# Selective scan on one NeuronCore: the PSUM tiles of a unit's transposed products as two one-bank halves, four in turn

## The chip, the cores and the metric

The kernel runs on one core of a Trainium2 chip. The metric is the device time of one execution in microseconds (us), taken as the median of several runs. Profile lines name the engines as PE (TensorE matmul), PEld (TensorE weight load), DVE (VectorE), ACT (ScalarE), POOL (GpSimd) and SP (the queue that issues the DMAs); L1633 is line 1633 of the kernel.

## What is computed

The input is a batch of 8 images of 64 x 64 positions and 192 channels, fp32. Layer 0 is a Mamba-like block with convolutions, a chunked state-space sum and an MLP; the change does not touch it. Layer 1 is a two-dimensional selective scan. Cut to what matters, for each image, each of 4 directions k, each of 384 channels d and each of 16 states n:

```
delta = softplus(dts + bias)                  # [4096 positions, 384]
dA    = exp(delta[..., None] * A[None])
dBu   = (delta * u)[..., None] * bm[:, :, None, :]
h     = dA * h + dBu                          # one position after another, 4096 of them
y     = sum over n of h * cm
```

Directions 0 and 2 go through the image by rows, forward and backward, 1 and 3 by columns. The four results are added, normalised, gated and projected, and the result is added to the layer's input.

## The kernel before

**Order of the program.** `tile_kernel` runs layer 0 for all images and then layer 1. `layer1` treats the images one after another. For each it runs first the "front" of this image (normalisation, projection, depthwise convolution, and the first pieces of its scan) beside the "finish" of the image before; the order of that part comes from a small planner (`Flow`) that gives each step a cost and a due time. Then it runs `main()` of `scan`, whose order is written out by hand: every instruction that goes through `o(...)` keeps program order on its engine.

**Tiling of the scan.** The 4096 positions of a direction are cut into 8 chunks of TT = 512. A step s is one chunk of one direction: 32 steps for an image. The 16 states are handled as NP1 = 8 pairs p, and the 384 channels as DT = 3 blocks d of 128. A unit u is one (s, p, d): 24 units in a step, 768 in an image, 6144 in all. A tile of a unit has 128 partitions, which are 2 states x 64 channels, and two halves f = 0, 1, one for each 64 channels of block d; each half is 512 positions long.

**What a unit does, engine by engine.**

- ScalarE: `decay` (L1606) writes ea = exp(delta x A), 2 instructions of 128 x 512, one for each f. `weigh` (L1591) writes pw, the products delta x u x B with the positions on partitions, 8 instructions for each (s, p), handed out 3, 3, 2 to the units d = 0, 1, 2, and ten instructions ahead of their use.
- TensorE: `supply` (L1617) turns pw round, 8 transposes of 128 x 128: four (j) for half 0 and then four for half 1. They go into the PSUM tile g. `collect` (L1662, with L1660 for the first pair of direction 0) sums the states of the unit before into the PSUM tile y of its channel block.
- VectorE: `run` (L1633) scans, 2 instructions of 128 x 512, one for each f. Each reads ea from SBUF and g from PSUM and writes hs. `add` (L1671, L1673) takes y into the image's sum after the last pair.
- GpSimd: a small copy cy (L1645) keeps the last column as the start of the next step, and hc = hs x C (L1647), one instruction of 128 x 1024, is what `collect` reads.
- SP: the DMAs that repeat delta (dr) and C (cb) over the partitions, and the loads for the next step (xc, ut).

**The loop.** In `main`, iteration u issues in this order: run(u), decay(u + 2), the 2 or 3 weigh of this iteration, supply(u + 1), collect(u - 1), add(u - 2), and then the pieces of `prepare` for the next step that are due at this unit. Those pieces (delta, its transposes p_du and p_b, the projections p_d at L1480, the copies xdbl at L1487 and bt at L1503, and softplus spa at L1516 and L1517) are dealt out by a table over the unit's place in the step: p_d at 2, 3 and 4, xdbl at 5, p_b at 6, and so on.

**Buffers.** The pool of ea (e1) has 3 buffers, so decay(u + 2) takes the one that run(u - 1) read. hs and hc have 3 each, y has one for each of three channel blocks. In PSUM, [...]y takes 3 banks, the tile of `prepare` takes 1, and g takes 4: two tiles of two banks each. The tile g is `[128, 2, TT]` fp32, 4 KiB a partition, so half 0 lies in one bank and half 1 in the next. A tile's buffer is handed on when its readers are done with it; all waits between engines are derived from what reads and writes which tile.

Of the kernel before, what the change touches and what calls it, by code (L numbers as in the profile page):

```python
# [8 lines left out]
F32 = mybir.dt.float32  # L9
AF = mybir.ActivationFunctionType  # L10
ALU = mybir.AluOpType
PSUM = bass.MemoryType.PSUM
# [5 lines left out]
TT = 512  # L18
# [35 lines left out]
def bc(ap, axis, shape):  # L54

    return ap.unsqueeze(axis).to_broadcast(shape)
# [975 lines left out]
def layer1(tc, consts, x1s, mv1, out, w_in, w_x, w_dt, w_out):  # L1032
# [3 lines left out]
    kw = v["kw"].rearrange("p (t k) -> p t k", t=DT)  # L1036
# [3 lines left out]
    with ExitStack() as ctx:  # L1040
# [393 lines left out]
        def scan(xo):  # L1434
# [5 lines left out]
            pools, ready = {}, {}  # L1440

            def spool(name, bufs, **kw):
                pools[name] = cx.enter_context(tc.tile_pool(name=name, bufs=bufs, reuse_waits="tile", **kw))
# [4 lines left out]
            made = {}  # L1448

            def first(s):  # L1450
                return steps[s][1] == (0 if steps[s][0] < 2 else NS1 - 1)
# [123 lines left out]
            def load_c(s, p):  # L1575
                state[s]["cb", p] = cb = pools["bc1"].tile([128, TT], F32, name="cb")
                for i in range(2):
                    o(
                        nc.sync.dma_start(
                            out=cb[i * 64 : i * 64 + 64], in_=state[s]["cd"][2 * p + i].partition_broadcast(64)  # L1580
                        )
                    )

            def weigh(s, p, j, i):

                st = state[s]
                if i == 0:
                    st["pw", p, j] = pools["pw1"].tile([128, 2 * DT, 2, 64], F32, name="pw")
                n = 2 * p + i
                o(  # L1590
                    nc.scalar.activation(  # L1591
                        st["pw", p, j][:, :, i],
                        st["duT"][:, j].rearrange("p (g c) -> p g c", c=64),
                        AF.Copy,
                        scale=st["bt"][:, j, n : n + 1],
                    )
                )

            def decay(u):
                s, p, d = units[u]  # L1600
                k, c = steps[s]
                made["e", u] = ea = pools["e1"].tile([128, 2, TT], F32, name="ea")
                for f in range(2):
                    at = 2 * d + f
                    o(
                        nc.scalar.activation(  # L1606
                            ea[:, f], state[s]["dr", d][:, f], AF.Exp, scale=an[:, k, p, at : at + 1]
                        )
                    )

            def supply(u):
                s, p, d = units[u]
                made["g", u] = g = pools["g1"].tile([128, 2, TT], F32, name="g")
                for f in range(2):
                    for j in range(NB1):
                        o(
                            nc.tensor.transpose(  # L1617
                                g[:, f, j * 128 : j * 128 + 128],
                                state[s]["pw", p, j][:, 2 * d + f].rearrange("p a b -> p (a b)"),
                                ident,  # L1620
                            )
                        )

            def run(u):
                s, p, d = units[u]
                k, c = steps[s]
                st = state[s]
                ea, g = made.pop(("e", u)), made.pop(("g", u))
                h = pools["h1"].tile([128, 2, TT], F32, name="hs")
                rev = (lambda ap: ap) if k < 2 else (lambda ap: ap[:, ::-1])  # L1630
                for f in range(2):
                    o(
                        nc.vector.tensor_tensor_scan(  # L1633
                            rev(h[:, f]),
                            rev(ea[:, f]),
                            rev(g[:, f]),
                            0.0 if first(s) else state[s - 1]["cy"][:, p, d, f : f + 1],
                            ALU.mult,
                            ALU.add,
                        )  # L1640
                    )
                if "cy" not in st:
                    st["cy"] = pools["pr1"].tile([128, NP1, DT, 2], F32, name="cy")
                last = TT - 1 if k < 2 else 0
                o(nc.gpsimd.tensor_copy(st["cy"][:, p, d], h[:, :, last]))  # L1645
                made["hc", u] = hc = pools["h1"].tile([128, 2, TT], F32, name="hc")
                o(nc.gpsimd.tensor_mul(hc, h, bc(st["cb", p], 1, [128, 2, TT])))  # L1647

            def collect(u):
                s, p, d = units[u]  # L1650
                k, c = steps[s]
                st = state[s]
                if p == 0:
                    st["y", d] = pools["y1"].tile([128, TT], F32, name=f"y{d}")
                y = st["y", d]
                hc = made.pop(("hc", u))
                half = [slice(f * 64, f * 64 + 64) for f in range(2)]
                if p == 0 and k == 0:
                    for f in range(2):
                        o(nc.tensor.matmul(y[half[f]], dskip[:, d, half[f]], st["xc"][:, d], start=True, stop=False))  # L1660
                for f in range(2):
                    o(nc.tensor.matmul(y[half[f]], sel, hc[:, f], start=p == 0 and k > 0, stop=p == NP1 - 1))  # L1662

            def add(u):
                s, p, d = units[u]
                k, c = steps[s]
                if p == NP1 - 1:
                    ya = view(yacc, k, d, c * TT, TT)
                    yv = seq(state[s]["y", d], k)
                    if k == 0:  # L1670
                        o(nc.vector.tensor_copy(ya, yv))  # L1671
                    else:
                        o(nc.vector.tensor_add(ya, ya, yv))  # L1673
# [51 lines left out]
                f.at["du", d] = r  # L1725

            def main():
                for name, n, kw in (("h1", 3, {}), ("y1", 1, dict(space=PSUM)), ("g1", 2, dict(space=PSUM))):
                    spool(name, n, **kw)
                supply(0)  # L1730
                rest = iter(todo[10:])
                nu = len(units)
                for u, (s, p, d) in enumerate(units):
                    if p == 0 and d == 0:
                        pieces = prepare(s + 1) if s + 1 < len(steps) else {}
                    s2, p2 = (s, p + 1) if p < NP1 - 1 else (s + 1, 0)
                    if s2 < len(steps) and d == 0:
                        load_c(s2, p2)
                    run(u)
                    if u + 2 < nu:  # L1740
                        decay(u + 2)
                    for _ in range((3, 3, 2)[d]):
                        if t := next(rest, None):
                            weigh(*t)
                    if u + 1 < nu:
                        supply(u + 1)
                    if u >= 1:
                        collect(u - 1)
                    if u >= 2:
                        add(u - 2)  # L1750
                    for f, *args in pieces.get(p * DT + d, ()):
                        f(*args)
                collect(nu - 1)
                add(nu - 2)
                add(nu - 1)
                cx.close()
# [7 lines left out]
        for b in range(nb + 1):  # L1764

            f = Flow(tc, after=True)
# [126 lines left out]
```

## Time and profile before

| | |
|---|---|
| three runs, us | 23690.56, 23702.0, 23706.31 |
| median | 23702.0 |
| span of the profiled execution | 23706.3 (the highest of the three runs, to the tenth) |
| layer 0 | 0 to about 5000 us of the span |
| scan of one image, first transpose to last y (image 4 of 0 to 7) | 2105.9 |
| finish of an image and front of the next, between two scans | about 240 |
| ACT busy in that scan | 2079.1 |
| DVE busy in that scan | 2007.6 |
| POOL busy in that scan | 1918.6 |
| PE busy in that scan | 1864.9 |

A group's line in the profile gives source line, engine, operation, tiles written and read, shape, count, then busy us and mean ns of one, then the idle time of the engine just before these instructions and who ended most of it. A line of the order of time gives start, length, engine, line, operation, tiles and count, and in brackets the idle time before it with its releaser. A line of waits reads: who waited for whom, us in total, times, longest. Busy time of instructions that overlap on one engine is counted once in a busy table, but each keeps its own length in a mean.

### The profile page before, as it was taken

How to read it: one execution, taken by the hardware profiler on the slowest of the kernel's cores; microseconds unless marked ns; L12 is line 12 of the kernel's file. 1: busy time of each engine (PE TensorE's matmuls, PEld its weight loads, DVE VectorE, ACT ScalarE, POOL GpSimd, SP SyncE). 2: the span in 40 equal slices, each digit the busy share in tenths (PEclk: the TensorE clock that was granted, in tenths of full speed). 3: DMA queues.
4: the chain of work that ended last, by engine and by line, in shares of the span. 5: the costliest groups of instructions: out<-in, count | busy, mean ns of one | idle time of the engine just before them, and what ended most of it. 6: DMA issues, size and time to landing. Idle time of an engine off the chain costs nothing.

```text
span 23706.3 us, 312102 instructions
## 1 busy us (share of the span) xinstructions
PE 21012.6 (89%) x100356; PEld 10233.4 (43%) x100356; DVE 21257.2 (90%) x22093; ACT 20961.7 (88%) x37466; POOL 16001.1 (67%) x12871
## 2 busy tenths in 40 slices
PE   8999999978888888888888888888888888888888
PEld 4444444434444444444444444444444444444444
DVE  7888888779998999899989998999899989998998
ACT  5666666679998999899989998999899989998998
POOL 1111111159995998599859986997699769976997
PEclk8999999989999999999999999999999999999999
DMA  1111111133233322332233233322333333333332
GB/s 51 44 44 44 45 45 46 36 101 81 82 78 112 81 81 77 110 82 81 77 108 81 81 80 111 81 81 78 108 81 82 84 102 81 82 86 100 82 82 67
DMA packets 1205983, 1859.70 MB, mean 78 GB/s; under 512 B 268960, under 2 KB 502336, under 8 KB 1195136
## 3 DMA queue, kind: packets, MB, share of 16 engines
q1 hardware_dynamic: 1204352, 1839.73, 28.5%
q8 instruction: 807, 13.22, 0.2%
q14 instruction: 824, 6.75, 0.1%
HBM read 1225.98 MB, written 210.50 MB: 61 GB/s over the span
## 4 chain that ended last, share of the span: by engine, by line
POOL 46%; PE 22%; ACT 13%; DVE 8%; issue 6%; DMA 3%; SPq 1%; POOLq 0%; ACTq 0%; DVEq 0%
POOL hc L1647 43%; ACT pw L1591 5%; ACT ea L1606 5%; POOL cy L1645 3%; PE p_f L955 3%; DVE xs L1201 2%; DMA xc<-xo 2%; PE p_x L448 2%; PE p_f L975 2%; PE y L1662 2%; PE p_o L872 1%; PE g L1617 1%; PE p_y L789 1%; PE p_d L1480 1%; PE p_z L531 1%
## 5 line engine op out<-in xcount | busy, mean ns | idle before, releaser
L1647 POOL TENSOR_TENSOR hc<-hs,cb 128x1024 f32<-128x1024 f32 x6144 | 14577.6, 2373 | 12.3 <-POOL cy L1645 10.5
L1633 DVE TENSOR_TENSOR_SCAN hs<-ea,cy,g 128x512 f32<-128x512 f32 x10752 | 13027.1, 1262 | 602.4 <-PE g L1617 408.7
L1591 ACT ACTIVATE pw<-duT,bt 128x384 f32<-128x384 f32 x16384 | 8875.4, 601 | 23.5 <-DVE duT L1538 23.5
L1606 ACT ACTIVATE ea<-dr,an 128x512 f32<-128x512 f32 x12288 | 8121.7, 709 | 186.9 <-DVE hs L1633 169.5
L1662 PE MATMUL y<-hc,sel 128*64 128x512 f32 x24576 | 6628.6, 618 | 1836.3 <-POOL hc L1647 1816.1
L1617 PEld LDWEIGHTS g<-ident,pw 128*128 128x128 f32 x49152 | 5288.2, 141 | 4335.1 <-issue 2666.3
L1617 PE MATMUL g<-ident,pw 128*128 128x128 f32 x49152 | 6788.1, 279 | 60.8 <-ACT pw L1591 29.3
L1645 POOL COPY cy<-hs 128x2 f32<-128x2 f32 x6144 | 1150.7, 187 | 3394.4 <-DMA out_x<-xl 1744.8
L1662 PEld LDWEIGHTS y<-hc,sel 128*64 128x64 f32 x24576 | 1226.6, 135 | 3250.6 <-POOL hc L1647 3025.0
L1633 DVE TENSOR_TENSOR_SCAN hs<-ea,g 128x512 f32<-128x512 f32 x1536 | 1764.2, 1203 | 160.9 <-PE g L1617 119.6
L365 POOL TENSOR_TENSOR s<-xs 96x512 f32<-96x512 f32 x64 | 121.7, 1902 | 2136.0 <-DVE xs L343 1846.6
L1201 DVE SCALAR_TENSOR_TENSOR xs<-pad,p,xs 128x4096 f32<-128x4096 f32 x192 | 860.9, 4484 | 48.0 <-ACT xs L1191 40.8
L1509 PE MATMUL p_dt<-xdbl,wd 13*128 13x512 f32 x1536 | 857.5, 639 | 41.8 <-DVE de L1522 39.9
L365 POOL TENSOR_TENSOR s<-sq 96x512 f32<-96x512 f32 x128 | 180.4, 1409 | 937.9 <-ACT sq L378 842.3
L1480 PE MATMUL p_d<-xc,wx 128*44 128x512 f32 x1536 | 788.7, 596 | 23.4 <-DMA xc<-xo 23.4
L343 DVE SCALAR_TENSOR_TENSOR x<-xx,p,x 96x512 f32<-96x512 f32 x1024 | 784.4, 815 | 15.2 <-ACT x L332 15.0
L955 PE MATMUL p_f<-h,wf 96*128 96x512 f32 x1536 | 757.2, 631 | 43.8 <-ACT zs L550 27.4
L343 DVE SCALAR_TENSOR_TENSOR xs<-xin,p,xs 96x512 f32<-96x512 f32 x1024 | 746.9, 768 | 3.6 <-ACT xs L332 3.6
L975 PE MATMUL p_f<-m,wf 128*96 128x512 f32 x1536 | 695.0, 603 | 0.0
L1531 PEld LDWEIGHTS p_du<-ident,de 128*128 128x128 f32 x3072 | 323.4, 141 | 610.1 <-DVE de L1522 406.3
L365 POOL TENSOR_TENSOR s<-x 96x512 f32<-96x512 f32 x64 | 109.1, 1704 | 690.3 <-DVE x L343 606.7
L448 PE MATMUL p_x<-h,wi 96*128 96x512 f32 x1024 | 559.4, 679 | 12.0 <-ACT h L405 12.0
(202 smaller groups left out, 19293.3 us busy)
## 6 DMA issues: line engine op xcount, KB each, us to landing
cb<-cd SPq DMA_DIRECT2D x4096, 128.0 KB
dr<-de SPq DMA_DIRECT2D x3072, 128.0 KB
xc<-xo SPq DMA_DIRECT2D x256, 768.0 KB
e<-csd SPq DMA_DIRECT2D x256, 384.0 KB
xl<-x SPq DMA_DIRECT2D x256, 384.0 KB
ut<-xo SPq DMA_DIRECT2D x128, 768.0 KB
ut<-xo SPq DMA_DIRECT2D x256, 384.0 KB
xo<-xs SPq DMA_DIRECT2D x48, 1024.0 KB
```

What stands on the lines that cost most here:

```text
L343: nc.vector.scalar_tensor_tensor(im(out[:, ct]), tap(ct, j), w[:, ct, j : j + 1], im(out[:, ct]), ALU.mult, ALU.add)
L448: nc.tensor.matmul(ps, wi[:, ct, 390 + mt * 128 : 518 + mt * 128], h[:, ct], start=ct == 0, stop=ct == 1)
L955: nc.tensor.matmul(ps, wf1[:, ct, mt * 128 : mt * 128 + 128], h[:, ct], start=ct == 0, stop=ct == 1)
L975: nc.tensor.matmul(ps[:CP], wf2[:, kt, ct * CP : ct * CP + CP], m[:, kt], start=kt == 0, stop=kt == 5)
L1201: nc.vector.scalar_tensor_tensor(xs, tap(j), kw[:, d, j : j + 1], xs, ALU.mult, ALU.add)
L1591: nc.scalar.activation(st["pw", p, j][:, :, i], st["duT"][:, j].rearrange("p (g c) -> p g c", c=64), AF.Copy, scale=st["bt"][:, j, n : n + 1],
L1606: nc.scalar.activation(ea[:, f], state[s]["dr", d][:, f], AF.Exp, scale=an[:, k, p, at : at + 1])
L1617: nc.tensor.transpose(g[:, f, j * 128 : j * 128 + 128], state[s]["pw", p, j][:, 2 * d + f].rearrange("p a b -> p (a b)"), ident,)
L1633: nc.vector.tensor_tensor_scan(rev(h[:, f]), rev(ea[:, f]), rev(g[:, f]), 0.0 if first(s) else state[s - 1]["cy"][:, p, d, f : f + 1], ALU ...
L1645: o(nc.gpsimd.tensor_copy(st["cy"][:, p, d], h[:, :, last]))
L1647: o(nc.gpsimd.tensor_mul(hc, h, bc(st["cb", p], 1, [128, 2, TT])))
L1662: o(nc.tensor.matmul(y[half[f]], sel, hc[:, f], start=p == 0 and k > 0, stop=p == NP1 - 1))
```

## The change

The pool g1 gets four buffers for two, and a unit takes two tiles `[128, TT]` (one bank each), one for each half, for one tile `[128, 2, TT]`. With four in turn, half f of unit u + 1 takes the buffer that half f of unit u - 1 had. The tile of half 1 is asked for after the transposes of half 0 have been issued. `run` takes a list of the two tiles. The number and order of instructions on each engine, their shapes and the four banks stay.

```diff
             def supply(u):
                 s, p, d = units[u]
-                made["g", u] = g = pools["g1"].tile([128, 2, TT], F32, name="g")
                 for f in range(2):
+                    made["g", u, f] = g = pools["g1"].tile([128, TT], F32, name="g")
                     for j in range(NB1):
                         o(
                             nc.tensor.transpose(
-                                g[:, f, j * 128 : j * 128 + 128],
+                                g[:, j * 128 : j * 128 + 128],
                                 state[s]["pw", p, j][:, 2 * d + f].rearrange("p a b -> p (a b)"),
                                 ident,
                             )
...
-                ea, g = made.pop(("e", u)), made.pop(("g", u))
+                ea, g = made.pop(("e", u)), [made.pop(("g", u, f)) for f in range(2)]
                 h = pools["h1"].tile([128, 2, TT], F32, name="hs")
                 rev = (lambda ap: ap) if k < 2 else (lambda ap: ap[:, ::-1])
                 for f in range(2):
...
                             rev(ea[:, f]),
-                            rev(g[:, f]),
+                            rev(g[f]),
                             0.0 if first(s) else state[s - 1]["cy"][:, p, d, f : f + 1],
...
-                for name, n, kw in (("h1", 3, {}), ("y1", 1, dict(space=PSUM)), ("g1", 2, dict(space=PSUM))):
+                for name, n, kw in (("h1", 3, {}), ("y1", 1, dict(space=PSUM)), ("g1", 4, dict(space=PSUM))):
```

## The prediction, made before the run

> **What bounds the kernel now.** I read the groups of the page first, then the busy table cut at step boundaries, then ScalarE's waits, then the order of time around one wait.
>
> The groups (line, engine, operation, tiles, count | busy us, mean ns | idle before, releaser):
>
> ```profile
> L1633 DVE TENSOR_TENSOR_SCAN hs<-ea,cy,g 128x512 f32<-128x512 f32 x10752 | 13027.1, 1262 | 602.4 <-PE g L1617 408.7
> L1591 ACT ACTIVATE pw<-duT,bt 128x384 f32<-128x384 f32 x16384 | 8875.4, 601 | 23.5 <-DVE duT L1538 23.5
> L1606 ACT ACTIVATE ea<-dr,an 128x512 f32<-128x512 f32 x12288 | 8121.7, 709 | 186.9 <-DVE hs L1633 169.5
> L1617 PE MATMUL g<-ident,pw 128*128 128x128 f32 x49152 | 6788.1, 279 | 60.8 <-ACT pw L1591 29.3
> ```
>
> VectorE waits for the transposed products (g) 408.7 us in all, and ScalarE waits for the scan (hs) 169.5 us. The question is which of the two sets the end. The busy table answers it (columns: PE, PE loads, DVE, ACT, POOL busy us, clock, DMA). I cut it from the ea of unit 14 of one step to that of the next: a step of direction 0, the step into direction 1, a later one.
>
> ```profile
> 7463.10:7529.59 66.49, 60.21 (x329) 29.21 (x330) 63.18 (x60) 65.35 (x120) 59.88 (x49) 1.00 0.28 80
> 7862.10:7927.35 65.25, 58.17 (x321) 28.88 (x321) 62.34 (x61) 65.15 (x120) 60.32 (x49) 1.00 0.34 82
> 8123.78:8189.29 65.51, 57.80 (x317) 28.47 (x318) 63.17 (x60) 65.33 (x119) 59.88 (x49) 1.00 0.32 82
> ```
>
> ScalarE bounds the scan: it is busy 65.15 of 65.25 us where it never waits, so **65.25 us is the floor of a step** with this ScalarE work. The other two steps are 1.24 and 0.26 us above it. Only that excess can be won; VectorE's 63 of 65.5 us is cover, not the bound. ScalarE's wait:
>
> ```profile
> ACT ea L1606 <- DVE hs L1633: 169.5, 102, 12.8
> ```
>
> Most of the 169.5 us is one wait of some 12.6 us in each image's first step, while TensorE still finishes the image before; the change doesn't touch that. The rest is the excess. One such wait, in step 1 of image 4:
>
> ```profile
> 12137.72 1.09 PE L1617 MATMUL g<-ident,pw 128*128 128x128 f32 x8
> ...
> 12138.95 2.45 DVE L1633 TENSOR_TENSOR_SCAN hs<-ea,cy,g 128x512 f32<-128x512 f32 x2 [0.79 <-PE g L1617]
> ...
> 12141.46 1.09 PE L1617 MATMUL g<-ident,pw 128*128 128x128 f32 x8
> ...
> 12142.69 2.45 DVE L1633 TENSOR_TENSOR_SCAN hs<-ea,cy,g 128x512 f32<-128x512 f32 x2 [1.29 <-ACT ea L1606]
> ...
> 12145.06 0.66 DVE L1487 COPY xdbl<-p_d 44x512 f32<-44x512 f32 x1
> 12145.17 1.33 ACT L1606 ACTIVATE ea<-dr,an 128x512 f32<-128x512 f32 x2 [0.97 <-DVE hs L1633]
> ```
>
> The eight transposes of unit 5 end at 12141.46 + 1.09 = 12142.55; both scans run from 12142.69 to 12145.14; the ea of unit 8, which takes the buffer that these scans read, starts at 12145.17, 0.97 us late. (The releaser named at 12142.69 is wrong: that unit's ea is older, and g ended 0.14 us before, as for unit 4.) So the first scan, which reads only half 0 of g, waited until half 1 was written too. Over all units that waited on g, the first scan starts 0.135 us after the eighth transpose, never after the fourth.
>
> **What the Trainium skill says.** "PSUM — Partial Sum Buffer", Terms, gives a bank as 2 KiB per partition (512 fp32) and forbids two engines on one bank and quadrant at once. A half tile is just one bank, so VectorE reads one while TensorE writes another; a unit's two halves already lie in two banks, so nothing here is newly shared. The trace agrees so far as its scans read while transposes of the next unit are written. "VectorE: DVE Perf Modes", Two Vector instructions with no wait between them, says that a wait which the sequencer handles alone does not hold up the next instruction. The trace agrees: four scans in a row took 4.79 us where 4 x 1.262 = 5.05, an overlap of 0.085 at each joint, also at the joint with an EVENT_SEMAPHORE (50 ns, one for nearly every unit now: 6137). "TensorE: Matmul & The Clock Gate", The cost: per-tile semaphore tail, says that matmuls end in order and that signals queue at 26 ns each. No run here shows that price.
>
> **The change part by part.**
>
> 1. *The first scan no longer waits for half 1.* Start times of single transposes: the first step is 0.165 us, the later six 0.109. Half 1 is thus 4 x 0.109 = **0.436 us**, and a first scan that waits on g starts up to that much earlier. The second scan starts 1.19 us after the first, when half 1 is long there.
>
>    Direction 0, steps 1 to 7 of each image: 66.50 us each (median over the images). The chain is the last pw of the second state pair, then TensorE without a gap for 8.3 us (dskip, y and p_d matmuls between the transposes), then the scans of unit 5, then ea. Only its last link gets shorter, by 0.436; the remaining 0.8 of the 1.25 stays, because TensorE is late next. 7 x 0.436 = 3.05 us an image.
>
>    Directions 1 to 3: 23 steps, of which three stand at 65.25, three at 65.34 and the others at about 65.56, some up to 65.9. There, too, units 4 and 5 wait on g (0.44 and 0.49 us by the trace), then the scans and a copy run in a row to unit 6, whose buffer ea of unit 9 needs. The visible idle there is only 0.08 us; the start-to-start times of pw and ea show the rest: 0.506 without a wait, 0.607 and 0.678 for these two, together 0.27 (a waited instruction loses its 0.1 us overlap). The shift of 0.436 covers that, so the step falls to the floor. Summing excess over 65.25, capped at 0.436, over all eight images: 48 us, 6.0 an image. It is 5.2 from the usual steps and 0.8 from the longer ones.
>
>    First step of an image: the first scan waits 0.18 us on g behind a copy, and gains that; the scan of unit 5 then gains 0.436 as above. 0.6 an image. End: the last six scans run in a row from one that waited 0.37 us on g; 0.36 an image.
>
>    Sum: 3.05 + 6.0 + 0.6 + 0.36 = 10.0 us an image, **80 us** for eight.
>
> 2. *Half 0 comes free after the first scan.* TensorE's transposes waited on the scan 8 times for 12.5 us in all, once an image: the third unit's, 1.64 us. Half 0 could start there about 1.2 us sooner, but y of unit 0 behind it waits for POOL's hc anyway. Cover gone, it would be 8 x 1.2 = 10 us; I take 0.
>
> 3. *The second scan needs a wait on TensorE of its own.* It now waits only for ea. Two waits make another EVENT_SEMAPHORE, 50 ns. Behind it in VectorE's queue are all later scans, and POOL's hc and ScalarE's ea wait for those. It is read while the first scan runs; I take 0. Upper bound: 0.05 plus the lost overlap 0.084 = 0.134 a unit. It can't be below 0.
>
> 4. *TensorE: a second wait and a second signal per unit.* Behind the wait stand half 1, then y. The wait is for a scan two units back, done unless the unit is among the 8 above. Units whose transposes wait on four pw tiles run eight in 1.09 us like the others, so a satisfied wait is free. Upper bound: 0.056 each, as at the first step of a unit (0.165 less 0.109). In direction 0 three supplies lie in the chain: 0.17 off 0.436, or 7 x 8 x 0.17 = 9 us. I take 0. The signal, at the skill's 26 ns, lies behind 0.135 us of latency per scan: up to 7 x 8 x 0.026 = 1.5 us, taken as 0.
>
> 5. *Space* is the same (four banks), and no step, DMA or order moves. Everything in part 1 removes a wait from an unchanged order on in-order engines; that alone can't make anything start later.
>
> The profiled execution's span is 23706.3 us, the same as the highest of the three runs (23706.31), so nothing lies around it; the median is 23702.0, 4.3 lower. 23706.3 - 80 = 23626; on the median, **23622 us**.
>
> **The rivals.**
>
> - *Only visible idle comes back.* If the lost overlap of 0.2 us a step stays, directions 1 to 3 give what the idle itself sums to, 19 us, not 48: 24 + 19 + 5 + 3 = 51 us, 23651. For it: idle is what a profile shows. Against: the step with no wait reaches 65.25 with the same instructions.
> - *The scan still waits for both halves*, because the signal is still given after the eighth transpose: 23702. For it: in the kernel before the halves were already in separate banks and it waited all the same. Against: the halves become separate tiles, and waits elsewhere go by tile.
> - *Slower: the wait of part 3 isn't hidden.* At 0.134 us a unit VectorE needs 24 x 0.134 = 3.2 us more a step, on 63.2 busy and some 0.7 of g waits left: 67.1. That is 1.6 above 65.5 for 23 steps and 0.6 above 66.5 for 8: (37 + 5) x 8 = 340 us, 24040. It is slower from about (65.5 - 63.9) / 24 = 0.07 us a unit. Against: the overlap that survives a sequencer wait today.
> - *More*: the 10 us of part 2 and uncapped long steps (3 us): 23609.
>
> **How the numbers follow.** The forecast 0.70 (23605 to 23640 by the bounds of parts 2 and 4), visible idle only 0.12, both halves 0.08, slower 0.06, more 0.04. A difference of 0.2% (47 us), about what a measurement of this kernel can tell from no change, lies at 23655. Faster by over it: 0.70 + 0.04 and half of the 0.12 rival or a little less, 0.79. Slower by over it 0.06; within, 0.15. The range goes from 23605 to 23672: forecast, more (nearly) and visible idle, with the bounds.
>
> **What would show it.** Scans that start about 0.135 us after a fourth transpose; direction-0 steps at 66.06 us; later steps at 65.25 with ScalarE's wait on the scan gone but for the first step; VectorE's EVENT_SEMAPHOREs near 12,288 with scans still overlapping by 0.085. Wrong if two scans of a unit lose that overlap, if first scans still start after the eighth transpose, or if later steps stay at 65.5 though scans start sooner: then something else holds ScalarE.

## The result, and the profile after

| | before | after |
|---|---|---|
| median, us (5 runs each) | 23702.0 | 23620.3 |
| ratio of after to before, 95% interval | | 0.9962 [0.9949, 0.9976] |
| span of the profiled execution | 23706.3 | 23594.7 |

The changed kernel is 0.38% faster by the ratio; 23622 was forecast. One of its five runs had a mean TensorE clock of 0.61 and took 35113.5 us; it is left out of the ratio, but not of the median, which without it is 23613.2. The gain is thus 88.8 us, with an interval from some 57 to 121 us; by the median in the table it would be 81.7.

The two profiled spans differ by 111.6 us, more than the medians. So I split them at the same instructions, summed over the eight images (the parts are given to a tenth, so sums can be off by one in the last digit). A step is measured as in the prediction, from the first ea of its unit 14 to that of the next.

| part of the span, us | before | after | difference | forecast |
|---|---|---|---|---|
| layer 0, to the first transpose of layer 1 | 5004.8 | 4982.0 | -22.8 | 0 |
| start of a scan to unit 14 of its first step | 301.4 | 296.5 | -5.0 | -5 |
| direction 0, 7 steps each | 3724.4 | 3700.1 | -24.4 | -24 |
| directions 1 to 3, 23 steps each | 12055.5 | 12004.5 | -51.0 | -48 |
| last step | 503.7 | 503.6 | -0.1 | 0 |
| from there to the last y of a scan | 267.8 | 263.9 | -3.9 | -3 |
| between scans, and after the last | 1848.8 | 1844.3 | -4.6 | 0 |

The scans give 84.3 us. Layer 0 has the same instructions in both kernels; in the profiled executions of the ten experiments it took 4988 to 5016 us. So I take its 22.8 us as scatter between executions, and compare kernels below by step times and by medians of runs. The median of each of the 31 steps of an image agrees within 0.02 us between the kernel before and experiment 1, which runs at the same speed.

The busy table of the changed kernel, for the same three steps as before (columns: PE, PE loads, DVE, ACT, POOL busy us, clock, DMA):

```profile
7429.72:7495.79 66.07, 60.54 (x330) 29.26 (x329) 62.91 (x60) 65.37 (x119) 59.85 (x49) 1.00 0.31 81
7826.15:7891.40 65.25, 59.15 (x326) 29.20 (x323) 61.92 (x60) 65.15 (x120) 60.62 (x49) 1.00 0.32 82
8087.11:8152.35 65.24, 58.44 (x318) 28.40 (x316) 63.04 (x60) 65.14 (x119) 59.83 (x49) 1.00 0.33 82
```

Direction 0 went from 66.50 to 66.07 and the later step from 65.51 to 65.24, with ScalarE busy for 65.14 of it: it stands on the floor. All 23 later steps of all images do (65.22 to 65.26); the steps that stood at 65.25 did not move.

The order of time at the place the prediction quotes (step 1 of the fourth image, which is image 3 where the first is image 0; units 4, 5 and 8):

```profile
12081.31 1.09 PE L1617 MATMUL g<-ident,pw 128*128 128x128 f32 x8
...
12082.11 2.45 DVE L1633 TENSOR_TENSOR_SCAN hs<-ea,cy,g 128x512 f32<-128x512 f32 x2 [0.82 <-PE g L1617]
...
12085.06 1.09 PE L1617 MATMUL g<-ident,pw 128*128 128x128 f32 x8
...
12085.85 2.45 DVE L1633 TENSOR_TENSOR_SCAN hs<-ea,cy,g 128x512 f32<-128x512 f32 x2 [1.29 <-PE g L1617]
...
12088.34 1.33 ACT L1606 ACTIVATE ea<-dr,an 128x512 f32<-128x512 f32 x2 [0.53 <-DVE hs L1633]
```

The first scan now starts 0.80 us after the first of its unit's eight transposes, where it took 1.23 (12137.72 to 12138.95), and before the eighth ends. It is so wherever the first scan of a unit waited on g: 602 did, and started 0.135 us after the fourth transpose ended (median); before, 788 did, and started 0.136 us after the eighth. ScalarE's wait at unit 8 fell from 0.97 to 0.53. The two scans still run together in 2.45 us. VectorE's own wait on g (0.82, was 0.79) did not shrink: the scans of unit 3 had finished sooner too, 0.02 us before the first transpose of unit 4, where before it was 0.44 after it. That is why one reads a step's length, not the wait.

The groups, the waits of ScalarE, and the EVENT_SEMAPHOREs on VectorE's sequencer at L1633 (these are waits of the scans; the three numbers are shortest, median and longest, in ns):

```profile
L1633 DVE TENSOR_TENSOR_SCAN hs<-ea,cy,g 128x512 f32<-128x512 f32 x10752 | 12939.0, 1261 | 381.4 <-PE g L1617 356.9
...
L1606 ACT ACTIVATE ea<-dr,an 128x512 f32<-128x512 f32 x12288 | 8118.4, 709 | 137.0 <-DVE hs L1633 132.5
```

```profile
ACT ea L1606 <- DVE hs L1633: 132.5, 79, 12.6
```

```profile
L1633 DVEq EVENT_SEMAPHORE  x11523: 21/21/1271, 4985.6 to 23453.8; - x199
```

The same in the kernel before:

```profile
L1633 DVEq EVENT_SEMAPHORE  x6137: 21/50/1654, 5009.2 to 23566.1; - x198
```

The added waits are there (11523 for 6137), and cost nothing that can be seen: a scan keeps its 1261 ns, and the two scans of a unit overlap by 0.084 us in the median, with a wait between them (3053 units) as without (3091).

What VectorE waited for g, and TensorE for GpSimd's hc, before:

```profile
DVE hs L1633 <- PE g L1617: 528.3, 788, 3.5
...
PE y L1662 <- POOL hc L1647: 1816.1, 3496, 1.4
```

and after:

```profile
DVE hs L1633 <- PE g L1617: 433.3, 602, 3.2
...
PE y L1662 <- POOL hc L1647: 1167.2, 2301, 1.6
```

### The profile page after: what moved, and what is told of

Its sections match the earlier page's. It is cut to its first block, busy times and chain, and to the rows that moved or that the text cites. A ratio compares the mean times of both kernels' runs of the same rounds, so it can differ in the third digit from the quotient of the medians.

```text
span 23594.7 us, 314377 instructions
## 1 busy us (share of the span) xinstructions
PE 21129.1 (90%) x100356; PEld 10211.3 (43%) x100356; DVE 21205.1 (90%) x22093; ACT 20933.3 (89%) x37466; POOL 15970.7 (68%) x12871
## 4 chain that ended last, share of the span: by engine, by line
ACT 55%; PE 22%; POOL 9%; DVE 7%; issue 4%; DMA 2%; SPq 1%; POOLq 0%; ACTq 0%; DVEq 0%
ACT pw L1591 27%; ACT ea L1606 23%; POOL hc L1647 8%; PE p_f L955 3%; DVE xs L1201 2%; PE p_x L448 2%; PE p_f L975 2%; ACT spa L1517 2%; PE g L1617 2%; PE p_o L872 1%; ACT spa L1516 1%; PE p_y L789 1%; PE y L1662 1%; PE p_z L531 1%; PE p_o L1407 1%
## 5 line engine op out<-in xcount | busy, mean ns | idle before, releaser
L1633 DVE TENSOR_TENSOR_SCAN hs<-ea,cy,g 128x512 f32<-128x512 f32 x10752 | 12939.0, 1261 | 381.4 <-PE g L1617 356.9
L1606 ACT ACTIVATE ea<-dr,an 128x512 f32<-128x512 f32 x12288 | 8118.4, 709 | 137.0 <-DVE hs L1633 132.5
L1617 PE MATMUL g<-ident,pw 128*128 128x128 f32 x49152 | 6991.4, 280 | 414.2 <-ACT pw L1591 394.9
L1633 DVE TENSOR_TENSOR_SCAN hs<-ea,g 128x512 f32<-128x512 f32 x1536 | 1759.4, 1202 | 113.9 <-PE g L1617 76.4
L1522 DVE SCALAR_TENSOR_TENSOR de<-spa,p_dt 128x512 f32<-128x512 f32 x768 | 520.0, 677 | 240.1 <-ACT spa L1517 240.0
```

Of the source, the lines that this page charges most:

```text
L1606: nc.scalar.activation(ea[:, f], state[s]["dr", d][:, f], AF.Exp, scale=an[:, k, p, at : at + 1])
L1617: nc.tensor.transpose(g[:, j * 128 : j * 128 + 128], state[s]["pw", p, j][:, 2 * d + f].rearrange("p a b -> p (a b)"), ident,)
L1633: nc.vector.tensor_tensor_scan(rev(h[:, f]), rev(ea[:, f]), rev(g[f]), 0.0 if first(s) else state[s - 1]["cy"][:, p, d, f : f + 1], ALU.mu ...
```

## The experiments

All edits are on the changed kernel unless it says otherwise, and are cut to what matters. Each ratio is to the kernel before, run beside the experiment. Step times are medians over the eight images, for the usual step of direction 0 and the usual later one; the kernel before has 66.50 and 65.56, the changed one 66.07 and 65.24.

**1. Half 1 first.** Is it the first scan's wait, or that buffers come free by halves?

```diff
-                for f in range(2):
+                for f in (1, 0):
                     made["g", u, f] = g = pools["g1"].tile([128, TT], F32, name="g")
```

> Keeps the four half tiles, their separate hand-on and the added waits, but issues the transposes of half 1 before those of half 0, so that the first scan is ready only after the eighth transpose again. Theory (the first scan used to wait for half 1): the whole gain is gone, 23702 within 15 us, direction-0 steps back at 66.5 and the usual later steps at 65.5 to 65.6. Rival (buffers that come free half by half, four in turn, are what helped): stays at about 23620, steps at 66.07 and 65.24.

Measured: ratio to the kernel before 0.9999 [0.9990, 1.0008]; steps 66.50 and 65.56. Its direction-0 and later steps, and the place of unit 5 and unit 8:

```profile
7473.61:7540.11 66.50, 60.22 (x331) 29.25 (x330) 63.20 (x60) 65.36 (x119) 59.89 (x49) 1.00 0.29 80
...
8134.22:8199.75 65.53, 57.78 (x319) 28.47 (x318) 63.19 (x60) 65.35 (x119) 59.89 (x49) 1.00 0.31 82
```

```profile
12154.89 1.09 PE L1617 MATMUL g<-ident,pw 128*128 128x128 f32 x8
...
12156.12 2.45 DVE L1633 TENSOR_TENSOR_SCAN hs<-ea,cy,g 128x512 f32<-128x512 f32 x2 [1.29 <-ACT ea L1606]
...
12158.61 1.33 ACT L1606 ACTIVATE ea<-dr,an 128x512 f32<-128x512 f32 x2 [0.96 <-DVE hs L1633]
```

The scan starts 1.23 us after the first transpose again and ScalarE waits 0.96. Half tiles, four in turn, hand-on by halves, all as in the change, and the gain is gone. So the gain hangs on the order of half 0 and half 1 against the scans. One thing is not as in the change, though the expectation says so: the added waits on VectorE are gone too, since the half that the second scan reads is now written first.

```profile
L1633 DVEq EVENT_SEMAPHORE  x6137: 21/50/2520, 5018.5 to 23578.6; - x198
```

So this run says nothing on what the added waits cost.

**2. Transposes in pairs.** Both half tiles are now asked for ahead of the transposes.

```diff
                 for f in range(2):
-                    made["g", u, f] = g = pools["g1"].tile([128, TT], F32, name="g")
-                    for j in range(NB1):
+                    made["g", u, f] = pools["g1"].tile([128, TT], F32, name="g")
+                for j in range(NB1):
+                    for f in range(2):
...
```

> Transposes issued in pairs, block j of half 0 and then block j of half 1, so that half 0 is written after the seventh transpose. Theory: a unit whose pw are all there gains only 0.109 us for its first scan. But a unit with d = 0 that waits for the last pw has two transposes left after it, not five, so that what stands behind it on TensorE starts 0.33 us sooner: direction-0 steps 66.50 - 0.33 - 0.11 = 66.06, later steps near the floor (65.25 to 65.3). About 23620 to 23630. Rival (only the place of the fourth transpose counts): 66.39 and about 65.45, 23675.

Measured: 0.9960 [0.9945, 0.9974], median 23621.5; steps 66.07 and 65.24. The time came as the theory had it, and excludes the rival's 66.39. It stands on two effects that happen to sum to the change's, so experiments 6 and 7 take them apart.

**3. Three halves in turn.**

```diff
-                for name, n, kw in (("h1", 3, {}), ("y1", 1, dict(space=PSUM)), ("g1", 4, dict(space=PSUM))):
+                for name, n, kw in (("h1", 3, {}), ("y1", 1, dict(space=PSUM)), ("g1", 3, dict(space=PSUM))):
```

> The changed kernel with three half tiles in turn, not four. Half 1 of a unit then takes the buffer that half 0 of the unit just before it had, so its transposes wait for that unit's first scan. Theory (number of buffers and early hand-on don't matter, the separate wait does): steps stay at 66.07 and 65.24, about 23620; at most a few waits of TensorE of under 1 us. Rival (hand-on matters): slower than 23650.

Measured: 0.9957 [0.9942, 0.9971], median 23611.7; steps 66.06 and 65.24. TensorE does wait for scans now:

```profile
PE g L1617 <- DVE hs L1633: 190.1, 308, 0.7
```

These 190 us (12.5 in the kernel before, 4.6 in the changed one) are cover: no step got longer. One bank of PSUM comes free at no cost.

**4. Pieces for the next step one unit later.**

```diff
-                    2: [(project, 0)],
-                    3: [(project, 1)],
...
-                    17: [(keep_du, 2)],
+                    3: [(project, 0)],
+                    4: [(project, 1)],
...
+                    18: [(keep_du, 2)],
```

> The changed kernel with the pieces for the next step (p_d projections to the last product) one unit later each. In direction 0 one p_d projection (0.86 us of TensorE) then falls behind the transposes of unit 5. Theory (after the change TensorE's gapless run is what is left of the excess, 66.07 - 65.25 = 0.82): direction-0 steps fall to the floor of 65.25 to 65.3, others stay; 23620 - 7 x 8 x 0.82 = 23574. Rival (VectorE or POOL holds direction 0 next): steps stay above 65.8, 23605 or more.

Measured: 0.9940 [0.9925, 0.9955], median 23575.2; direction 0 at 65.43, later steps at 65.24. The time is as forecast, the step not quite: 0.64 of the 0.83 us that were left in direction 0 are gone, and 0.19 stays. The edit moves VectorE's copy xdbl and all later pieces too, so this run alone does not say how much of the 0.64 was TensorE's gapless run; experiment 7 shows that the run alone gives 0.33. In the start-to-start times of ScalarE the 0.19 shows as two lost overlaps of 0.08 and 0.09 us, at units 10 and 11.

**5. Two halves in turn.**

```diff
-                for name, n, kw in (("h1", 3, {}), ("y1", 1, dict(space=PSUM)), ("g1", 4, dict(space=PSUM))):
+                for name, n, kw in (("h1", 3, {}), ("y1", 1, dict(space=PSUM)), ("g1", 2, dict(space=PSUM))):
```

> The changed kernel with only two half tiles, one for each half. The transposes of half 0 for the next unit then wait for the first scan of this unit, those of half 1 for its second. Theory (VectorE needs the next half 0 only 1.2 us after it gives the buffer back, and four transposes take 0.44): most units lose nothing; where p_d or dskip matmuls stand behind the late half 1, units 2 to 5 of a step, up to 0.5 us of VectorE, part of it seen by ScalarE: steps 65.3 to 65.6 and about 66.3, 23640 to 23720. Rival (buffers in turn are what the change is about): clearly slower than the kernel before, 23800 or more.

Measured: 1.0133 [1.0119, 1.0146], median 24021.0; steps 68.64 and 66.93. A miss: slower than I allowed, and the rival's sign. What VectorE and ScalarE wait for in it:

```profile
DVE hs L1633 <- PE g L1617: 882.0, 1458, 2.4
```

```profile
ACT ea L1606 <- DVE hs L1633: 387.6, 547, 12.5
```

VectorE waits on g 882 us (433 in the changed kernel). I had looked only at what VectorE needs. The transposes of half 1 must now wait for the second scan of the unit before, and TensorE, in order, keeps y, p_d and the next unit's half 0 behind them: in step 11 of the fifth image half 1 of units 1, 2, 3 and 7 ends 1.17 us after its half 0 instead of 0.44, and the scans of units 4, 5 and 8 then wait 0.95, 0.43 and 0.33 us for g. So the number of buffers does matter, down to two; three are enough.

**6. Pairs for all units with d = 0.** The pair order of experiment 2 where d = 0, half after half where not.

```diff
-                    made["g", u, f] = g = pools["g1"].tile([128, TT], F32, name="g")
-                    for j in range(NB1):
...
+                    made["g", u, f] = pools["g1"].tile([128, TT], F32, name="g")
+                fs, js = range(2), range(NB1)
+                for f, j in [(f, j) for j in js for f in fs] if d == 0 else [(f, j) for f in fs for j in js]:
...
```

> The changed kernel, transposes in pairs (block j of both halves) for units with d = 0 only, half after half for the others. Theory: TensorE's gapless run of direction 0 starts 3 x 0.109 = 0.33 us sooner after the last pw, and units 4 and 5 keep their 0.436: direction-0 steps 66.07 - 0.33 = 65.74, later steps at 65.24: 23620 - 18 = 23602. Rival (VectorE or POOL is next in direction 0): 66.07, 23620.

Measured: 0.9959 [0.9946, 0.9973], median 23611.6; direction 0 at 65.99: not 65.74 as expected, nor the rival's 66.07. ScalarE's wait at unit 8 fell from 0.53 to 0.21, as the theory had it, but one of 0.32 stood at unit 9, where there had been 0.07.

**7. Pairs for one unit.** This run tests why. The edit is shown against experiment 6.

```diff
-                for f, j in [(f, j) for j in js for f in fs] if d == 0 else [(f, j) for f in fs for j in js]:
+                for f, j in [(f, j) for j in js for f in fs] if (p, d) == (1, 0) else [(f, j) for f in fs for j in js]:
```

> The changed kernel, transposes in pairs for one unit of a step only, the one with p = 1, d = 0, at which TensorE's gapless run of direction 0 starts. The run with pairs for all d = 0 units took 0.32 us off ScalarE's wait at unit 8 but put 0.25 on at unit 9, whose buffer the scans of unit 6 read, and unit 6 has d = 0 too. Theory: with unit 6 half after half, the gain of 0.33 stays: direction-0 steps 65.72 to 65.76, 18 us less than the changed kernel. Rival (something else holds unit 9): 65.99 again.

Measured: 0.9951 [0.9934, 0.9968], median 23590.4; direction 0 at 65.74. As forecast. Both effects of experiment 2 are thereby seen apart: 0.33 us of TensorE's run that starts at unit 3, and 0.25 us more a step where unit 6 has the pair order too (experiment 6: its first scan follows the seventh transpose, not the fourth), 0.33 where all units have it (experiment 2).

**8. Experiments 4 and 6 together.**

```diff
-                    2: [(project, 0)],
...
+                    3: [(project, 0)],
...
-                    made["g", u, f] = g = pools["g1"].tile([128, TT], F32, name="g")
-                    for j in range(NB1):
...
+                    made["g", u, f] = pools["g1"].tile([128, TT], F32, name="g")
+                fs, js = range(2), range(NB1)
+                for f, j in [(f, j) for j in js for f in fs] if d == 0 else [(f, j) for f in fs for j in js]:
...
```

> The changed kernel with both: pairs for units with d = 0, and the pieces for the next step one unit later. Theory: what is left of the excess in direction 0 (65.43 - 65.24 = 0.19) is still the same run of TensorE, so it goes: all steps at 65.24 to 65.3, 23575 - 10 = 23565. Rival: 65.43 stays, 23575.

Measured: 0.9944 [0.9930, 0.9957], median 23573.2; steps 65.43 and 65.24. The rival's numbers: with the pieces moved, starting the run of unit 3 sooner gives nothing, so it is no longer what holds direction 0. This and experiment 4 are the fastest versions here that keep the whole computation; they can't be told apart.

**9. What stands next behind ScalarE.** The kernel of experiment 8 without the second softplus instruction: it leaves out the log, so delta is exp(x) in the scan. The edit is shown against experiment 8.

```diff
                     o(nc.scalar.activation(a, st["p_dt", d], AF.Exp))
-                    o(nc.scalar.activation(a, a, AF.Ln, bias=1.0))
```

> As the run before it, but the second ScalarE instruction of softplus (Ln, three in a step) is left out, so delta is exp(x) in the scan. ScalarE does 3 x 0.54 to 0.61, about 1.7 us less a step. Theory (ScalarE alone sets the floor now): steps fall until VectorE holds them, which is busy some 63.1 us a step and has about 0.7 us of waits left: 63.6 to 64.2, 23565 - 8 x 31 x 1.4 = about 23220. Rival (VectorE or POOL already stands next to ScalarE): steps fall by less than 0.5 us, 23440 or more.

Measured: 0.9883 [0.9870, 0.9897], median 23428.4; steps 65.14 and 64.85. The rival was nearer. A later step of it (one of 65.01, somewhat longer than the usual 64.85), then what ScalarE and VectorE wait for (in this kernel L1605 is the ea of L1606):

```profile
8059.52:8124.53 65.01, 57.42 (x318) 28.52 (x316) 63.00 (x60) 63.91 (x116) 60.05 (x50) 1.00 0.33 83
```

```profile
ACT ea L1605 <- DVE hs L1633: 311.3, 721, 12.6
```

```profile
DVE hs L1633 <- PE g L1617: 569.5, 877, 2.4
```

ScalarE is busy 63.91 us and has idle time; VectorE is busy 63.0 and waits on g for the remaining 2. I had put those waits at 0.7 us. So ScalarE does hold the changed kernel, since a step shrank when its work did; but the chain of VectorE and its waits on g stands only 0.4 us a step behind it (65.24 less 64.85).

**10. The pieces later, in the kernel before.** The edit of experiment 4 with whole tiles g.

```diff
-                    2: [(project, 0)],
-                    3: [(project, 1)],
...
-                    17: [(keep_du, 2)],
+                    3: [(project, 0)],
+                    4: [(project, 1)],
...
+                    18: [(keep_du, 2)],
```

> The kernel before (whole tiles g), with only the pieces for the next step one unit later. Theory (both edits cut the same run of TensorE and scans in direction 0, and their cuts add; later steps need the split): direction-0 steps 66.50 - 0.64 = 65.86, later steps still about 65.55: 36 us less than before. Rival (moving the pieces does alone what the split does): later steps at 65.24.

Measured: 1.0006 [0.9997, 1.0014], median 23716.7; steps 65.90 and 65.9. Direction 0 came as expected (65.86), the later steps rose by 0.35, which neither side expected. In one such step ScalarE has three short waits on the scan (units 8, 9, 10) where it had one (unit 9), and VectorE waits on g four times, 2.7 us, where it did three times, 1.8. The same move that gives some 40 us after the change (23613.2 to 23575.2) gives none before it. With the split the later steps stay at ScalarE's floor, so there its cost does not show.

## Why the prediction was right

That the median of 23620.3 lies within 2 us of the forecast is in part luck: by the ratio the gain is 88.8 us, and the median of the kernel before alone was 23702 to 23712 from one round of runs to the next. The better test is the 84.3 us that the scans gained, for 80 forecast, and that the gain lies in the parts where it was put.

1. *The first scan no longer waits for half 1: shown.* The first scans follow the fourth transpose, as the result shows for all units that waited, and experiment 1 turns the order of the halves round and loses all of the gain. The size was right: direction-0 steps at 66.07 for a forecast 66.06, later steps at 65.24 for 65.25.
2. *Only ScalarE's excess counts: shown.* TensorE's wait for y on hc fell by 649 us between the profiles (lines above), and the scans by 84; what an engine that does not hold the step waits less is not time won. (VectorE's waits on g fell by 95, too near to 84 to tell.) And every later step, whatever it took before, ended at 65.22 to 65.26 and no lower. Experiment 9 shows that the floor is ScalarE's.
3. *The lost overlap comes back too: shown.* Rival one allowed 19 us in directions 1 to 3; 51 came. The term was a little low: I had capped each step at 0.436, giving 48, but the long steps of 65.7 to 65.9 all went to 65.24, 3 us more. In 22 of these 23 long steps ScalarE's ea waited longer on the scan than in the usual ones, 0.15 to 0.39 us (20 times at unit 8, twice at unit 9); what made the scan late there was not looked into.
4. *TensorE holds the rest of direction 0: shown for 0.33 of the 0.83 us* by experiment 7, which only starts its run sooner. Experiment 4 takes 0.64 off, but moves pieces of other engines as well, so beyond the 0.33 this is likely and not shown; what makes ScalarE late in the last 0.19 is open.
5. *The added waits are free: shown* as far as the steps on the floor and the kept overlap go; no run has the early first scan without them. The bounds of 0.134 and 0.056 us were too careful. 11523 EVENT_SEMAPHOREs stand for the 12,288 that I named: the count was a guess at one more for each unit. On TensorE, where I expected a second wait to cost 0.056 us at most, the fifth transpose follows the fourth in 0.109 us in 4667 of the 4685 units whose fourth did not itself have to wait.
6. *Hand-on by halves is worth nothing: shown* by experiment 1, which keeps it and gains nothing. Experiment 3 shows that even three halves are enough. My reason, that TensorE hardly ever waits for the scan, says nothing on how few buffers do; experiment 5 shows the edge.

The rival of both halves fell with the first scans, the slower one with the kept overlap. Its working had a weak term all the same, the 0.7 us of remaining waits on g, which were 2 in experiment 9. That run puts the chain of VectorE and its waits at 64.85 us, and so the threshold at about (65.56 - 64.85) / 24 = 0.03 us a unit and not 0.07. This is an estimate, since that kernel also has the pieces moved and pairs for d = 0; by it the change was nearer to that edge than I wrote.

## What to carry to other kernels

Where a consumer reads a tile in parts, give each part a tile of its own and write the part first that is read first; the gain is the time of writing the rest, and only where the consumer truly waits. Price it against the engine that sets the step (here ScalarE): take its shortest step with the same work as the floor, and count only the excess, including the overlap that each waited instruction loses. And ask how far the next chain stands behind: here 0.4 us a step, which decides what a second edit is worth.

## What the runs showed of the hardware

- A ScalarE ea whose scan came just in time or late lost up to 0.1 us beyond its visible idle, its overlap with the pw before it. In the kernel before, from that pw to the ea took 0.506 us start to start where nothing was late; in the usual later step it took 0.62 at unit 8 with an idle of 0.015, and 0.68 at unit 9 with one of 0.08 (medians). Of these 0.28 us a step only 0.09 was idle that a profile shows.
- An EVENT_SEMAPHORE (21 ns in the median after the change, 50 before it) on VectorE's sequencer left the overlap of 0.084 us between two scans as it was.
- Layer 0, with identical instructions, differed by up to 34 us between profiled executions (4982 to 5016), four tenths of the 84 us that the scans gained, while the median of each scan step repeated to 0.02 us between the kernel before and experiment 1.
